# A macaron block on one core: turns through TensorE or through DRAM, and the experts' second product in halves or whole

## The chip, the core and the metric

The kernel runs on one core of a Trainium2 chip. The core has TensorE (matrix products, PE in the profile), VectorE (DVE), ScalarE (ACT), GpSimd (POOL) and SyncE (SP), which issues all DMAs of this kernel. The metric is the device time of one execution in microseconds (us), median of several runs; lower is better.

## The reference

The input `x` has 8 batches of 256 tokens with 128 channels, in float32. Two layers are applied to it, each a half step of a feed-forward, a full step of attention and another half step (all on a normalized x):

```python
x = x + 0.5 * L0_ffn(norm(x))    # soft mixture of 16 experts with 64 slots each
x = x + L0_attn(norm(x))         # linear attention with elu + 1
x = x + 0.5 * L0_ffn(norm(x))    # the same experts again
x = x + 0.5 * L1_ffn(norm(x))    # gated unit with two hidden 512 x 512 products
x = x + L1_attn(norm(x))         # FAVOR+ attention, 16 heads, 32 random features
x = x + 0.5 * L1_ffn(norm(x))

# L0_ffn, with y = norm(x) * g + b and keys se = norm(slot_embeds):
logits = y @ se.T                           # per batch 256 tokens x 1024 slots
slots  = softmax(logits, over tokens).T @ y # 1024 slots x 128
eout   = (gelu(slots @ Wg + bg) * (slots @ Wu + bu)) @ Wd + bd   # per expert
out    = softmax(logits, over slots) @ eout

# FAVOR+: phi = exp(xw - max(xw)) * exp(-|x|^2 / 2) + eps, with xw = heads(x) @ proj
out = (phiQ @ (phiK.T @ V)) / (phiQ @ sum(phiK)), then @ Wo + bo
```

## The kernel before

All of x stays on chip. The batches form two groups of four; a group goes twice through `dispatch`, `experts` and `combine` (after the first time also through `linear`, the linear attention), then through `glu` (two batches at a time), `favor` and `glu` again. `group` (at the end of the kernel's function) writes this down batch by batch.

The order on the engines is not the written one. Each piece of work is a `step` with its engines and their expected costs in ns, the cells that it reads and writes, and a lag until its result can be used. `Plan.place` takes the steps greedily, that which can start first, with ties broken by a key (the TensorE work ahead of the step, plus a shift from the table `SHIFTS`, plus 45 us for the second group), gives out the buffers (`comb`, `slots`, `k1`, `k2`, `k4`, `we`, `sm`, and 8 PSUM banks `ps`) and so fixes each engine's order. SP is one of the engines of the plan: a DMA stands in SP's queue in the planned place and waits there for its data. Where the plan leaves TensorE idle before a step, `Plan.issue` puts in filler matmuls on the identity matrix (L1399 in the profile):

```python
            if s.idle > 700:
                idle(s.bank, int((s.idle - 300) / 224))
```

In `dispatch`, y comes from `norm`; `transposed` turns it (two flips, which are TensorE transposes against the identity, L375) and `affinely` scales it on the way out of PSUM. `replicated` writes y to DRAM in four pieces (L579) and reads it back in four copies of 32 partitions (L586), the layout in which `gathered` (L691) sums tokens into slots on four row tiles of TensorE. The maxima over all slots, which the second softmax needs, are turned (L375), reduced on VectorE (L719) and spread over the partitions by two more flips. GpSimd subtracts them (L737) and ScalarE takes the exponential (L743).

In `experts`, `fetch` brings an expert's matrices (L764) and, for every second expert, the biases of two (L767). `front` makes the gated hidden values (L787 on TensorE, L793, L798). `back` handles two experts at a time: the second product (L818) writes for each batch 64 slots of the first expert to partitions 0 to 63 and 64 slots of the second to 64 to 127, in half-width tiles. One VectorE instruction (L830) adds the bias and writes the result over the slots, where `combine` (L859) reads it.

`squares_turned` is another way to turn a matrix: VectorE transposes within 32 x 32 squares (L446), a DMA writes the result to DRAM (L449), and four DMAs read it back with the squares in turned places (L455). It serves in `linear` and `favor` for the normalized x, in `glu`, and in `favor` for the features of the queries. The attention's outputs in `project` and the FAVOR+ sums in `favor` are turned by flips and copied out of PSUM (L382 on ScalarE, L384 on VectorE).

## Time and profile before

| what | value |
|---|---|
| median of 3 runs | 740.42 us (740.34 to 740.69) |
| the profiled execution's own time | 743.85 us |
| its span, first to last instruction | 742.1 us |
| granted clock of TensorE | 0.998 |
| busy: TensorE, VectorE, ScalarE, GpSimd | 728.8, 517.2, 410.7, 306.1 us |
| DMA: packets, bytes, mean rate | 102105, 62.34 MB, 84 GB/s |
| 32 KB writes of y to DRAM (L579), 64 of them | 1.9 us to landing |
| 128 KB spills of squares (L449), 16 of them | 1.7 us to landing |
| 32 KB moves of squares back (L455), 64 of them | 2.3 us to landing |
| an expert's 384 KB (L764), 64 of them | 3.8 us to landing |

The busy time of an engine is the sum of its instructions' durations; for TensorE their ends are modelled, and the mean duration of a matmul is longer than its distance to the next. The distance between the starts of two groups in the time line is what a group costs.

### The profile page before, as it was taken

The numbers are of one execution on the slowest core, as the hardware profiler recorded it, in microseconds if no ns is written. First come the engines' busy times: TensorE is split into PE (matmuls) and PEld (weight loads), VectorE is DVE, ScalarE is ACT, GpSimd is POOL, SyncE is SP. The second block draws the span as 40 slices with busy tenths as digits, with TensorE's granted clock in tenths as the row PEclk, the third lists the DMA queues.
The fourth block names the chain that finished last, engine by engine and source line by source line (L and its number), as shares of the span: only waits on it lengthen the run. The fifth ranks groups of instructions, "written<-read, shape, count | busy, mean of one in ns | idle before, by whom it ended". The sixth has DMA issues, their size and how long they took to land.

```text
span 742.1 us, 15296 instructions
## 1 busy us (share of the span) xinstructions
PE 728.8 (98%) x5814; PEld 609.5 (82%) x5814; DVE 517.2 (70%) x1103; ACT 410.7 (55%) x774; POOL 306.1 (41%) x419
## 2 busy tenths in 40 slices
PE   8999999998999999999999999999999999999998
PEld 7878888997889988889878879788687677878787
DVE  6999965577868798975564274455998978855442
ACT  4889967257665577884553240433555664363331
POOL 7989446133427752459910022000745545211000
PEclk9999999999999999999999999999999999999999
DMA  5553432333330526333631210200344244120100
GB/s 143 150 140 118 139 93 94 109 81 97 126 114 2 146 83 197 99 94 119 171 99 52 85 29 1 57 0 15 78 114 95 42 118 81 32 60 14 42 1 29
DMA packets 102105, 62.34 MB, mean 84 GB/s; under 512 B 73104, under 2 KB 88848, under 8 KB 102032
## 3 DMA queue, kind: packets, MB, share of 16 engines
q1 hardware_dynamic: 102032, 61.36, 30.6%
q8 instruction: 46, 0.75, 0.4%
q14 instruction: 27, 0.22, 0.1%
HBM read 49.80 MB, written 11.53 MB: 83 GB/s over the span
## 4 chain that ended last, share of the span: by engine, by line
PE 87%; DVE 5%; DMA 3%; SPq 2%; issue 1%; POOL 1%; ACT 1%; POOLq 0%
PE ps L1077 27%; PE ps L787 14%; PE ps L818 8%; PE ps L859 8%; PE ps L691 6%; PE ps L615 4%; PE ps L1177 4%; PE ps L1147 4%; PE ps L1150 4%; PE ps L375 2%; DMA we<-in_We 1%; PE ps L1256 1%; DVE k L632 1%; PE ps L1307 1%; PE ps L1341 1%; PE ps L907 1%
## 5 line engine op out<-in xcount | busy, mean ns | idle before, releaser
L787 PE MATMUL ps<-slots,we 128*128 128x256 f32 x512 | 121.8, 384 | 4.0 <-DMA we<-in_We 2.3
L787 PEld LDWEIGHTS ps<-slots,we 128*128 128x128 f32 x512 | 94.7, 191 | 20.1 <-issue 5.2
L1077 PE MATMUL ps<-comb,slots 128*128 128x256 f32 x448 | 103.1, 381 | 0.0
L1077 PE MATMUL ps<-comb,comb 128*128 128x256 f32 x448 | 102.5, 381 | 0.0
L1077 PEld LDWEIGHTS ps<-comb,slots 128*128 128x128 f32 x448 | 83.6, 190 | 15.4 <-issue 3.9
L1077 PEld LDWEIGHTS ps<-comb,comb 128*128 128x128 f32 x448 | 83.6, 190 | 13.6 <-issue 2.5
L737 POOL TENSOR_TENSOR comb<-comb,k 128x1024 f32<-128x1024 f32 x32 | 75.1, 2369 | 33.5 <-DVE k L384 14.0
L793 ACT ACTIVATE k<-ps,small 128x256 f32<-128x256 f32 x128 | 56.5, 475 | 48.4 <-PE ps L787 46.1
L382 ACT COPY k<-ps 128x512 f32<-128x512 f32 (+2 forms) x55 | 28.5, 519 | 93.8 <-PE ps L1077 83.1
L670 POOL TENSOR_TENSOR comb<-comb,sm 128x1024 f32<-128x1024 f32 x32 | 60.9, 1911 | 41.4 <-DVE sm L665 41.4
L798 DVE SCALAR_TENSOR_TENSOR k<-ps,small,k 128x256 f32<-128x256 f32 x128 | 57.2, 475 | 29.2 <-ACT k L793 28.5
L412 POOL TENSOR_SCALAR sm<-sm 128x2 f32<-128x2 f32 x52 | 10.0, 193 | 153.1 <-DVE sm L406 140.1
L657 ACT ACTIVATE comb<-comb,sm 128x256 f32<-128x256 f32 x128 | 63.3, 497 | 13.7 <-PE ps L691 7.4
L1091 DVE TENSOR_TENSOR comb<-ps,k 128x512 f32<-128x512 f32 x48 | 32.9, 687 | 49.0 <-PE ps L1077 25.5
L818 PEld LDWEIGHTS ps<-we,k 128*64 128x64 f32 x1024 | 55.3, 137 | 9.2 <-issue 4.7
L615 PE MATMUL ps<-k,seT 128*128 128x256 f32 x256 | 61.7, 383 | 0.8 <-DVE k L495 0.5
L818 PE MATMUL ps<-we,k 128*64 128x128 f32 x1024 | 62.2, 275 | 0.0
L691 PE MATMUL ps<-comb,k 32*128 32x256 f32 x1024 | 59.9, 380 | 0.1
L859 PEld LDWEIGHTS ps<-slots,comb 128*128 128x128 f32 x512 | 58.4, 192 | 1.5 <-issue 1.3
L859 PE MATMUL ps<-slots,comb 128*128 128x129 f32 x512 | 59.6, 276 | 0.0
L1099 ACT ACTIVATE comb<-comb 128x512 f32<-128x512 f32 x48 | 30.0, 629 | 51.0 <-DVE comb L1091 50.8
L691 PEld LDWEIGHTS ps<-comb,k 32*128 32x128 f32 x1024 | 51.4, 185 | 5.6 <-issue 1.4
(144 smaller groups left out, 1303.7 us busy)
## 6 DMA issues: line engine op xcount, KB each, us to landing
we<-in_We SPq DMA_DIRECT2D x64, 384.0 KB, 3.8
k<-y SPq DMA_DIRECT2D x64, 128.0 KB, 2.9
t<-comb SPq DMA_DIRECT2D x8, 512.0 KB, 2.8
k<-t SPq DMA_DIRECT2D x32, 128.0 KB, 3.5
y<-k SPq DMA_DIRECT2D x64, 32.0 KB, 1.9
we<-in_bd SPq DMA_DIRECT2D x64, 32.0 KB, 3.6
t<-k SPq DMA_DIRECT2D x16, 128.0 KB, 1.7
k<-t SPq DMA_DIRECT2D x64, 32.0 KB, 2.3
```

The costliest lines, as they stand in the source:

```text
L615: mm(pl.ap[:, j, :], seT[:, 2 * u + j].rearrange("p k s -> p (k s)"), yt.ap, start=True, stop=True,)
L657: nc.scalar.activation(ex.ap[:, 4 * h + j, :], comb.ap[:, 4 * h + j, :], AF.Exp, bias=mx.ap[:, j : j + 1], accum_out=mx.ap[:, 4 + j : 5 + j],)
L670: nc.gpsimd.tensor_tensor(ex.ap[:, part], ex.ap[:, part], mx.ap[:, 8:12].unsqueeze(2).to_broadcast([P, 4, N]), ALU.mult,)
L691: mm(po.ap, yr.ap[rows, c, :], ex.ap[rows, :, 32 * c : 32 * c + 32], start=(c == 0), stop=(c == N // 32 - 1), tile_position=(32 * a, 0),)
L737: nc.gpsimd.tensor_tensor(raw, raw, mb.ap.unsqueeze(1).to_broadcast([P, 4, N]), ALU.subtract)
L787: mm(pe.ap[:, m, :], we.ap[:, ts(2 * m + c, P)], sl.ap[:, j, k, :, 0:S], start=True, stop=True,)
L793: nc.scalar.activation(ga.ap, pe.ap[:, 0, :], AF.Gelu, bias=bg[:, e, c : c + 1])
L798: nc.vector.scalar_tensor_tensor(ht.ap[:, c, :], pe.ap[:, 1, :], bu[:, e, c : c + 1], ga.ap, ALU.add, ALU.mult,)
L818: mm(po.ap[S * k : S * k + S, q, :], hts[k].ap[:, c, ts(q, S)], wes[k].ap[:, ts(4 + c, P)], start=(c == 0), stop=(c == 1), tile_position=( ...
L859: mm(po.ap[:, t, 0 : D + 1], comb.ap[:, j, ts(t, P)], eo()[:, j, q, 0 : D + 1], start=(j == 0), stop=(j == NJ - 1),)
L1077: mm(bank.ap[:, o], w(k)[:, c, ts(o, P)], rhs().rearrange("p (c n) -> p c n", c=2)[:, c, :], start=(start and o + c == 0), stop=(stop and ...
L1091: nc.vector.tensor_tensor(C(i, k)(), bank.ap.rearrange("p o n -> p (o n)"), other(), ALU.add)
```

## The change

- y in one spill: `replicated` writes y by one DMA of 128 partitions and reads it back in four as before, each in pieces of 1 KB instead of 4 KB; `gathered` picks its rows by another index.
- The experts' second product: one expert at a time, with two batches' slots side by side as a full 128-wide stationary side. Each expert's output is added to its bias into a buffer `moved`, and two DMAs place its halves over the slots (64 partitions each). The bias is now part of the matrix `We`, laid out by the host for all 128 partitions, and comes with the same DMA.
- Turns of the outputs in `project` and of the FAVOR+ sums: by `squares_turned`.
- The second layer's y: also by `squares_turned`, into a buffer of its own so that y stays for `replicated`, and scaled afterwards by `affinely`, now from the buffer and not from PSUM.
- The second layer's maxima (`last`): transposed in squares and reduced on VectorE, written to DRAM (4 KB), read back into all partitions (512 KB), and reduced again by two VectorE instructions.
- Costs and lags of SP's steps in the plan have other values, and `SHIFTS` is another table.

The second layer here means the second pass through the experts. The diff, without blank lines and most of `SHIFTS`:

```diff
--- before.py
+++ after.py
@@ -14,19 +14,18 @@
 P = 128
 SHIFTS = (
-    -2751, -1692, -1691, -12195, -784, -1588, -17523, -441, -1660, -895, -929, -659, -543, -591,
...
+    -1808, -823, -822, -570, -566, -619, -564, -372, -388, -402, -161, -439, -208, -237, -230,
...
 )
@@ -437,16 +436,16 @@
         )
         return y
-    def squares_turned(z, n, cells, dst, out):
-        flat = lambda: z()
+    def squares_turned(z, n, cells, dst, out, by=None):
         there = dram.tile([P, n // 32, 32], F32, tag=f"t{len(turns)}", name=f"t{len(turns)}")
         turns.append(there)
-        step({"DVE": 58 + 1.07 * n}, lambda _: nc.vector.transpose(z(), z()), cells, cells)
+        done, at = ([by], lambda: by.ap) if by else (cells, z)
+        step({"DVE": 58 + 1.07 * n}, lambda _: nc.vector.transpose(at(), z()), cells, done)
         def spill(_):
-            nc.sync.dma_start(there.rearrange("p k j -> p (k j)"), z())
+            nc.sync.dma_start(there.rearrange("p k j -> p (k j)"), at())
         def place(_):
@@ -457,8 +456,8 @@
                     squares[f],
                 )
-        step({"SP": 475}, spill, cells, [there.name], lag=1.5 * n)
-        step({"SP": 2000}, place, [there.name], out, lag=2.5 * n)
+        step({"SP": 335}, spill, done, [there.name], lag=1.1 * n - 850)
+        step({"SP": 2400 + 0.7 * n}, place, [there.name], out, lag=1.2 * n - 300)
     turns = []
@@ -469,7 +468,10 @@
             squares_turned(
                 lambda: y.ap[:, 0:n].rearrange("p t d -> p (t d)"), n * P,
                 [(y, t) for t in range(n)], lambda: yt.ap, [yt],
+                Buf("k1", (P, n * P)) if affine else None,
             )
+            if affine:
+                affinely(lambda: yt.ap, lambda: yt.ap, [yt], [yt], n * P, True)
             return yt
         pt = ps_(n, P)
@@ -485,7 +487,7 @@
             evacuated(lambda: yt.ap, flat, [pt], [yt], n * P)
         return yt
-    def affinely(dst, src, r, w, n):
+    def affinely(dst, src, r, w, n, port=False):
         def run(e):
@@ -494,7 +496,7 @@
             else:
                 nc.vector.tensor_scalar(dst(), src(), ng, nb, ALU.mult, ALU.add)
-        step({"ACT": act(n, True) + 87, "DVE": dve(n, 120)}, run, [*r, "ng"], w)
+        step({"ACT": act(n, True) + 87, "DVE": dve(n, 120)}, run, [*r, "ng"], w, port=port)
     def keys():
@@ -568,36 +570,36 @@
     dram = ctx.enter_context(tc.tile_pool(name="dram", bufs=1, space=bass.MemoryType.DRAM))
-    spilled = [dram.tile([32, N // 32, D], F32, tag=f"y{b}", name=f"y{b}") for b in range(B)]
+    spilled = [dram.tile([P, N], F32, tag=f"y{b}", name=f"y{b}") for b in range(B)]
     def replicated(y, b):
         yr = Buf("k4", (P, N // 32, D))
         def spill(_):
-            for k in range(4):
+            nc.sync.dma_start(spilled[b], y.ap.rearrange("p t d -> p (t d)"))
+        def spread(_):
+            blocks = spilled[b].rearrange("(k i) n -> i k n", k=4)
+            for a in range(4):
                 nc.sync.dma_start(
-                    spilled[b].rearrange("i (t k) d -> i k t d", k=4)[:, k],
-                    y.ap[32 * k : 32 * k + 32],
-                )
-        def spread(_):
-            for a in range(4):
-                nc.sync.dma_start(yr.ap[32 * a : 32 * a + 32], spilled[b])
-        step({"SP": 2500}, spill, [(y, t) for t in range(TT)], [("y", b)], lag=-1500)
-        step({"SP": 1765}, spread, [("y", b)], [yr], lag=900)
+                    yr.ap[32 * a : 32 * a + 32].rearrange("i (k t) d -> i k (t d)", t=TT), blocks
+                )
+        step({"SP": 335}, spill, [(y, t) for t in range(TT)], [("y", b)], lag=-500)
+        step({"SP": 1830}, spread, [("y", b)], [yr], lag=900)
         return yr
-    def dispatch(b, sl):
+    def dispatch(b, sl, last):
         plan.part()
         q = b % BG
         y = norm(b, True)
-        yt = transposed(y, TT, True)
+        yt = transposed(y, TT, True, squares=last)
         yr = replicated(y, b)
         if not loaded:
             key, plan.key = plan.key, 60000
@@ -689,7 +691,7 @@
                 for a, po in enumerate(pos):
                     rows = slice(32 * a, 32 * a + 32)
                     mm(
-                        po.ap, yr.ap[rows, c, :], ex.ap[rows, :, 32 * c : 32 * c + 32],
+                        po.ap, yr.ap[rows, TT * (c % 4) + c // 4, :], ex.ap[rows, :, 32 * c : 32 * c + 32],
                         start=(c == 0), stop=(c == N // 32 - 1), tile_position=(32 * a, 0),
                     )
@@ -708,27 +710,64 @@
             nc.vector.tensor_tensor(pm.ap[:, 0], pm.ap[:, 0], pm.ap[:, 1], ALU.max)
         step({"DVE": 330}, fold, [pm], [pm], port=True)
-        pt = ps_(TT, P)
-        mn = Buf("sm", (P, TT))
-        def turn_max(_):
-            for t in range(TT):
-                flip(pt.ap[:, t, :], pm.ap[:, 0, ts(t, P)])
-        def token_max(_):
-            nc.vector.tensor_reduce(mn.ap, pt.ap, AX.X, ALU.max)
-        step({"PE": flips(TT)}, turn_max, [pm], [pt])
-        step({"DVE": dve(N)}, token_max, [pt], [mn])
-        pb = ps_(N)
         mb = Buf("k1", (P, N))
-        def spread(_):
-            for t in range(TT):
-                flip(pb.ap[:, ts(t, P)], mn.ap[:, t : t + 1].to_broadcast([P, P]))
-        step({"PE": flips(TT)}, spread, [mn], [pb], takes=[mb])
-        evacuated(lambda: mb.ap, lambda: pb.ap, [pb], [mb], N)
+        if last:
+            there = dram.tile([P, N // 32], F32, tag=f"m{len(turns)}", name=f"m{len(turns)}")
+            turns.append(there)
+            mn, mr = Buf("sm", (P, N // 32)), Buf("k4", (P, 4, N))
+            def turn_max(_):
+                nc.vector.transpose(pm.ap[:, 0], pm.ap[:, 0])
+            def slot_max(_):
+                nc.vector.tensor_reduce(
+                    mn.ap, pm.ap[:, 0].rearrange("p (c s) -> p c s", s=32), AX.X, ALU.max
+                )
+            def spill(_):
+                nc.sync.dma_start(there, mn.ap)
+            def spread(_):
+                nc.sync.dma_start(
+                    mr.ap.rearrange("p a n -> p (a n)"),
+                    there.rearrange("p c -> (p c)").partition_broadcast(P),
+                )
+            def token_max(_):
+                nc.vector.tensor_tensor(mr.ap[:, 0:2], mr.ap[:, 0:2], mr.ap[:, 2:4], ALU.max)
+                nc.vector.tensor_tensor(
+                    mb.ap.rearrange("p (c i) -> p i c", i=32),
+                    *(mr.ap[:, a].rearrange("p (i c) -> p i c", i=32) for a in range(2)), ALU.max,
+                )
+            step({"DVE": dve(N)}, turn_max, [pm], [pm])
+            step({"DVE": dve(N)}, slot_max, [pm], [mn])
+            step({"SP": 335}, spill, [mn], [there.name], lag=-600)
+            step({"SP": 440}, spread, [there.name], [mr], lag=1300)
+            step({"DVE": 1060}, token_max, [mr], [mb], port=True)
+        else:
...
         for h in range(2):
             half = [(comb, 2 * h), (comb, 2 * h + 1)]
@@ -748,7 +787,7 @@
     def experts(sl):
         def whole(j):
-            return [(sl, j, q) for q in range(BG)]
+            return [(sl, j, k, q) for k in range(2) for q in range(BG)] + [(sl, j, "two")]
         filled = [(sl, "in", q, a) for q in range(BG) for a in range(4)]
@@ -761,18 +800,9 @@
             we = Buf("we", (P, 6 * P + D))
             def run(_):
-                nc.sync.dma_start(we.ap[:, 0 : 6 * P], i["We"][e])
-                if e % 2 == 0:
-                    for k in range(2):
-                        nc.sync.dma_start(
-                            we.ap[S * k : S * k + S, 6 * P :],
-                            i["bd"][e + k].partition_broadcast(S),
-                        )
-            step(
-                {"SP": 475 if e % 2 else 1400}, run, [(sl, "in", BG - 2, 0)], [we],
-                lag=1900 if e % 2 else 1000,
-            )
+                nc.sync.dma_start(we.ap, i["We"][e])
+            step({"SP": 475}, run, [(sl, "in", BG - 2, 0)], [we], lag=1500)
             return we
         def front(e, we):
@@ -807,46 +837,51 @@
                 step({"DVE": dve(256, 59)}, up, [pe, ga], [(ht, c)])
             return ht
-        def back(j, wes, hts):
-            po = ps_(BG, P)
+        def back(e, we, ht):
+            j, k = e // 2, e % 2
+            po = ps_(NB, P)
+            moved = Buf("k1", (P, NB, P))
             def down(_):
-                for q in range(BG):
+                for r in range(NB):
                     for c in range(2):
-                        for k in range(2):
-                            mm(
-                                po.ap[S * k : S * k + S, q, :], hts[k].ap[:, c, ts(q, S)],
-                                wes[k].ap[:, ts(4 + c, P)], start=(c == 0), stop=(c == 1),
-                                tile_position=(0, S * k),
-                            )
-            step(
-                {"PE": 1880}, down,
-                [*wes, *((ht, c) for ht in hts for c in range(2))], [po],
-            )
+                        mm(
+                            po.ap[:, r, :], ht.ap[:, c, ts(r, P)], we.ap[:, ts(4 + c, P)],
+                            start=(c == 0), stop=(c == 1),
+                        )
             def biased(_):
                 nc.vector.tensor_tensor(
-                    eo()[:, j, :, 0:D], po.ap,
-                    wes[0].ap[:, 6 * P :].unsqueeze(1).to_broadcast([P, BG, D]), ALU.add,
-                )
-            step({"DVE": dve(512)}, biased, [wes[0], po], whole(j))
+                    moved.ap, po.ap, we.ap[:, 6 * P :].unsqueeze(1).to_broadcast([P, NB, P]),
+                    ALU.add,
+                )
+            def place(_):
+                for h in range(2):
+                    nc.sync.dma_start(
+                        eo()[S * k : S * k + S, j, h::2, 0:D], moved.ap[S * h : S * h + S]
+                    )
             def twos(_):
                 nc.gpsimd.memset(eo()[:, j, :, D : D + 1], 2.0)
-            step({"POOL": 65}, twos, [], whole(j))
+            cells = [(sl, j, k, q) for q in range(BG)]
+            step({"PE": mms(*[P] * 4)}, down, [we, (ht, 0), (ht, 1)], [po], takes=[moved])
+            step({"DVE": dve(256)}, biased, [we, po], [moved])
+            step({"SP": 1340}, place, [moved], cells, lag=-300)
+            if k:
+                step({"POOL": 65}, twos, [], [(sl, j, "two")])
         got = []
         for e in range(E):
             plan.part()
             we = fetch(e)
             got.append((we, front(e, we)))
-            if e % 2 == 0 and e:
-                back(e // 2 - 1, *zip(*got[e - 2 : e]))
-        back(NJ - 1, *zip(*got[E - 2 :]))
+            if e:
+                back(e - 1, *got[e - 1])
+        back(E - 1, *got[E - 1])
         return eo
     def combine(b, comb, sl, eo):
@@ -863,7 +898,7 @@
             step(
                 {"PE": mms(*[D + 1] * NJ)}, gather,
-                [(comb, u) for u in range(4)] + [(sl, j, q) for j in range(NJ)], [(po, t)],
+                [(comb, u) for u in range(4)] + [c for j in range(NJ) for c in ((sl, j, 0, q), (sl, j, 1, q), (sl, j, "two"))], [(po, t)],
             )
         rc = Buf("sm", (P, TT))
@@ -887,15 +922,10 @@
     def project(b, oh, w):
-        pt = ps_(TT, P)
         ot = Buf("k1", (P, N))
-        def turn(_):
-            for t in range(TT):
-                flip(pt.ap[:, t, :], oh.ap[:, t, :])
-        step({"PE": flips(TT)}, turn, [oh], [pt], takes=[ot])
-        evacuated(lambda: ot.ap, lambda: pt.ap.rearrange("p t c -> p (t c)"), [pt], [ot], N)
+        squares_turned(
+            lambda: oh.ap.rearrange("p t d -> p (t d)"), N, [oh], lambda: ot.ap, [ot]
+        )
         projected_onto(b, ot, w)
     def projected_onto(b, ot, w):
@@ -1297,7 +1327,7 @@
             [(phi, 0, c) for c in range(4)],
             lambda: qk.ap.rearrange("p a b n -> p (a b n)"), [(qk, t) for t in range(TT)],
         )
-        pk, pkt = ps_(2, P), ps_(2, P)
+        pk = ps_(2, P)
         kvm = Buf("k1", (P, 2, P))
         def sums(_):
@@ -1317,17 +1347,13 @@
                 m4of.unsqueeze(1).unsqueeze(3).to_broadcast([P, 2, 4, M]), ALU.mult,
             )
-        def turn_sums(_):
-            for m in range(2):
-                flip(pkt.ap[:, m, :], kvm.ap[:, m, :])
         step(
             {"PE": 1020}, sums, [*((phi, 1, c) for c in range(4)), v1], [pk], takes=[kv, kvm]
         )
         step({"DVE": 340}, blocks, [pk], [kvm])
-        step({"PE": flips(2)}, turn_sums, [kvm], [pkt])
-        evacuated(
-            lambda: kv.ap, lambda: pkt.ap.rearrange("p a (c n) -> p a c n", c=4), [pkt], [kv], N
+        squares_turned(
+            lambda: kvm.ap.rearrange("p a n -> p (a n)"), N, [kvm],
+            lambda: kv.ap.rearrange("p a c n -> p (a c n)"), [kv],
         )
@@ -1367,7 +1393,7 @@
         bs_ = range(g * BG, (g + 1) * BG)
         for layer in range(2):
             sl = Buf("slots", (P, NJ, 2, BG, S1))
-            combs = {b: dispatch(b, sl) for b in bs_}
+            combs = {b: dispatch(b, sl, layer > 0) for b in bs_}
             eo = experts(sl)
             for b in bs_:
                 combine(b, combs[b], sl, eo)
@@ -1452,10 +1478,10 @@
                 get(f0 + "Wg"),
                 get(f0 + "Wu"),
                 wd.reshape(wd.shape[0], 2, P, P).transpose(0, 2, 1, 3).reshape(-1, P, 2 * P),
+                np.broadcast_to(get(f0 + "bd")[:, None, :], (wd.shape[0], P, P)),
             ],
             axis=2,
         ),
-        "bd": get(f0 + "bd"),
         "WqkvT": get("L0_attn_Wqkv").T,
         "WprojT": get("L0_attn_Wproj").T,
         "bproj": get("L0_attn_bproj"),
```

## The prediction

> **What bounds the kernel now.** I read the page's busy shares, then the chain that ended last, then the time line of TensorE group by group, then SyncE's queue, then the busy time by stage.
>
> The page and its chain of waits:
>
> ```profile
> PE 728.8 (98%) x5814; PEld 609.5 (82%) x5814; DVE 517.2 (70%) x1103; ACT 410.7 (55%) x774; POOL 306.1 (41%) x419
> ...
> PEclk9999999999999999999999999999999999999999
> ...
> PE 87%; DVE 5%; DMA 3%; SPq 2%; issue 1%; POOL 1%; ACT 1%; POOLq 0%
> ...
> L787 PE MATMUL ps<-slots,we 128*128 128x256 f32 x512 | 121.8, 384 | 4.0 <-DMA we<-in_We 2.3
> ```
>
> TensorE carries 87% of the chain at full clock. "98% busy" alone would not prove it, since ends of pipelined matmuls are modelled; the distance between starts does. From the time line of TensorE (start, us, engine, line, operation, count):
>
> ```profile
> 317.41 1.89 PE L787 MATMUL ps<-slots,we 128*128 128x256 f32 x8
> 319.14 0.38 PE L375 MATMUL ps<-ident,k 128*128 128x128 f32 x2
> 319.36 1.89 PE L787 MATMUL ps<-slots,we 128*128 128x256 f32 x8
> ...
> 354.93 5.34 PE L787 MATMUL ps<-slots,we 128*128 128x256 f32 x24
> 360.21 1.97 PE L818 MATMUL ps<-we,k 128*64 128x128 f32 x32
> 362.10 1.99 PE L787 MATMUL ps<-slots,we 128*128 128x256 f32 x8
> 363.94 1.03 PE L1147 MATMUL ps<-k,w1T 128*128 128x512 f32 x2
> ...
> 691.89 3.73 PE L1177 MATMUL ps<-w3T,comb 128*128 128x128 f32 x32
> 695.46 1.02 PE L1147 MATMUL ps<-k,w1T 128*128 128x512 f32 x2
> ```
>
> Prices, start to start: a 128x256 instruction is 1.73/8 = 0.216 us, a flip (transpose by matmul) 0.22/2 = 0.11, a full-array 128x128 instruction 3.57/32 = 0.112. (A full-array float32 matmul of the program is two instructions in the trace, a flip one.) The 32 instructions of the experts' second product (L818) take 1.89. The neighbours pay as well: the 24 before it take 5.28 instead of 24 x 0.216 = 5.18, the 8 after it 1.84 instead of 1.73, about 0.10 us on each side of a change of tile shape.
>
> With these prices and the program's order I add up TensorE. The full-array and narrow work without changes of shape is 701 us, of which 43 filler matmuls (L1399) are 9.6; 130 changes of shape at 0.10 are 13.0; another 0.08 for each of 28 visits to L818 (1.89 against 2 x 1.785 = 3.57 for two in a row, which the time line gives as 3.65) is 2.2. Total 716 of the span of 742.1. The other 26 us are 7 in the start-up before 61.6 us (9.6 of fillers stand there too), 1.6 before the first matmul, 3.3 after the last, and about 14 of small waits. The largest wait, again in the time line:
>
> ```profile
> 179.13 1.03 PE L787 MATMUL ps<-slots,we 128*128 128x256 f32 x4
> 182.32 1.46 PE L787 MATMUL ps<-slots,we 128*128 128x256 f32 x4 [2.17 <-DMA we<-in_We]
> 183.57 0.64 PE L375 MATMUL ps<-ident,k 128*128 128x128 f32 x2
> 184.00 1.92 PE L787 MATMUL ps<-slots,we 128*128 128x256 f32 x4
> 185.71 0.95 PE L972 MATMUL ps<-kv,k 128*128 128x129 f32 x4
> ```
>
> and SyncE's queue before it:
>
> ```profile
> 168.02 3.04 SPq L579 DMA_DIRECT2D y<-k  x4
> 171.56 2.58 SPq L455 DMA_DIRECT2D k<-t  x4
> 174.24 0.55 SPq L764 DMA_DIRECT2D we<-in_We  x1
> 174.83 1.16 SPq L767 DMA_DIRECT2D we<-in_bd  x2
> 176.03 0.58 SPq L764 DMA_DIRECT2D we<-in_We  x1
> ```
>
> An expert's weights were issued behind spills and square moves and came late. The wait is 2.2 us, but the eight 128x256 instructions and two flips around it then ran at up to twice their price (184.00 to 185.71 for four of them, 1.71 instead of 0.86): about 4 us in all. So an idle of 2 us costs two of slow matmuls on top.
>
> **The change, part by part.** TensorE first.
>
> Flips. Three turns go to squares through DRAM: the second layer's y (8 x 2 flips), the outputs in `project` (8 x 2), the FAVOR+ sums (8 x 2); and the second layer's maxima lose two flips to turn and two to spread (8 x 4). 80 flips x 0.109 = 8.7 us less.
>
> Second product. Before: 32 calls, each 32 half-width instructions, 1.785 us without the borders. After: 64 calls of 4 full-array matmuls, 8 instructions x 0.1117 = 0.893. That is 57.1 against 57.2: nothing by itself. The gain is the borders: in the order of the changed program the changes of shape fall from 130 to 89, 41 x 0.10 = 4.1, and the 28 x 0.08 = 2.2 go. 6.3 us less. The row first: 0.0558 us per half-width instruction, 0.1117 per full one, with equal work. The Trainium skill speaks against this edit: TensorEngine Tiling (Array Packing), Overview, "Theoretical Speedup", promises up to 2x from tiles where a dimension is at most 64, and the old form has 64 stationary columns. If that were a gain that is given up, the new form would cost twice, 57 us more. But the two batches' slots are now joined into one stationary side of 128 columns, so the array is as full as before; the sum by the rule's own premise is 0, and I take the row.
>
> Fillers. The plan puts 48 instead of 43, +5 x 0.223 = +1.1 us: 38 instead of 43 in the start-up, and three new places later (2, 5 and 3): before the first combine, between the first layer's linear attention and the experts, and before an expert's second product in the middle. Line 211 sets a filler count only where the plan idles over 0.7 us, and leaves 0.3 us each: +0.9.
>
> TensorE's sum: -8.7 - 6.3 + 1.1 + 0.9 = -13.0 us.
>
> SyncE's queue, in issue times. New: 128 placements of expert outputs, 64 rows each. No row has that shape; the nearest two are a 32 KB spill of 64 rows (0.593) and a square move (0.612), so between 0.33 (a 128-row spill) and 0.7, taken 0.67 for its 128 pieces: +86. 24 more spills at 0.33 and 96 more square moves at 0.62: +67. The maxima, 8 x (0.33 + 0.44): +6. y's spread in 1 KB pieces instead of 4 KB: 64 x 0.04 = +2. Gone: 64 bias loads at 0.58, -37 (the bias rides in `We`, 448 KB each instead of 384), and y's four spills become one, 16 x (2.4 - 0.33) = -33. In sum 238 us to 330. Between the first combine and the second layer's last one about 152 us of issuing fall into some 200 us, three quarters of the queue.
>
> Here the skill has a rule against the change: DMA: Bandwidth & Descriptors, "Rules for kernel authors": many small transfers should be joined, since under 64 KB one pays mostly overhead. The row agrees on the price (a 32 KB square move is 0.61 to issue and 2.3 to land, a 128 KB spill 0.33 and 1.7). Charged as elapsed time by the page's fixed cost of about 2 us, the net 152 added DMAs would be +304 us, an estimate. By the trace they overlap each other and TensorE, so only what arrives late counts; before, with 238 us of issuing, late `we` cost about 5 us (182 and 216 us).
>
> What is queued behind a placement: it waits for `biased` on VectorE, which waits for the second product, and the next experts' `we`, other batches' squares and y's spreads wait behind it on SP. Its reader is `gather` (L859 before), which needs all 16 experts. After the last second product of a stage, `biased` 0.42, two issues 1.3 and a landing of about 2 make 4 us where it was 0.7. The changed order puts L693 (3.67), other batches' glu or logits between, and the 2 fillers at the first combine: covered. If the cover is gone: four combines x 3.3 = 13 us.
>
> Latency of the squares: transpose 0.43, spill 0.33 + 1.7, four moves 2.5, landing 2.3 and, for y, the affine 0.55, some 8 us against 0.8 through PSUM, in 24 places. Covered by the other group's experts and by the glu (TensorE has no wait over 1 us from 300 on). The maxima take some 7 us longer and are due only at the combine.
>
> VectorE: the second product's add becomes 64 x 0.42 for 32 x 0.69, +5; transposes 24 x 0.43, +10; the maxima 8 x (0.43 + 0.41 + 1.3 - 0.41), the last pair bounded by 0.69 and by 0.61 each, +14; about half the copies out of PSUM go, -7. +22, to 539, 74%. The stage that matters:
>
> ```profile
> 0.00:61.60 61.60, 56.46 (x477) 47.29 (x478) 55.00 (x123) 44.33 (x123) 54.70 (x90) 1.00 0.59 158
> ...
> 190.00:300.00 110.00, 108.63 (x1008) 95.27 (x1008) 90.50 (x208) 76.17 (x160) 54.71 (x78) 1.00 0.38 109
> ```
>
> From 190 to 300 us VectorE (fifth number) works 90.5 of 110; about 9 to 10 of the 22 fall here, so 100 of the 106 that are left. Close, not over.
>
> In the start-up VectorE has 55 of 61.6 us, and the change takes nothing off it; y's single spill lands 2 us earlier. Gain 0 to 2, taken 0.5.
>
> New waits from a fuller SP queue and a tighter VectorE: at least -3 (the delay at 182 us stood behind four y spills, which shrink by 2.7 us), at most +16 (four like that at 182); taken +3, rather more than half of what `we` cost before.
>
> Sum: 742.1 - 13.0 - 0.5 + 3 = 731.6. The profiled execution took 743.85 with a span of 742.1; the median of the runs is 740.42, 1.7 below the span. So 730 us.
>
> **The rivals.**
> (a) VectorE is the bound from 190 to 300 us. It keeps that stage at 110 and passes some waits on, so the 4 us of TensorE saved there are lost and 2 to 3 more: 736. For it: 82% busy before. Against: 100 < 106, and the fillers planned there are only 8.
> (b) The gain is only exchanged for waits, 740: flips were cheap fill while TensorE waited. For it: fillers in three new places. Against: flips stand between matmuls without idle.
> (c) Slower: SP is the bound between the first combine and the second layer's last. Each in-order placement holds back `we`; when a `we` comes 2 us late, 4 us are lost, as at 182 us. It decides from four such events (16 us) on; five give 740.4 - 16 + 20 = 744. For it: three quarters full, placements that wait for VectorE in the same queue. Against: y's spills and the bias loads are out of that queue, and each weight has four buffers.
> (d) It doesn't do what it says: if the full-array product still drained at each border, the 6.3 would stay: 736.
>
> **How the numbers follow.** My forecast (725 to 734) 0.52, (a) or (d) 0.25, (b) 0.09, (c) 0.12, better than 725 0.02. 0.2% is 1.5 us, about what a measurement can tell from no change. Faster: 0.79; same: 0.09; slower: 0.12. The range reaches from 724 (fewer waits than before) to 741 (end of (b)) and leaves out (c) and a little below.
>
> **What would show it.** Right: 48 flips on k and 16 on sm; L850 with 8 instructions from start to start in 0.89 and the next 128x256 group at 0.216; TensorE's share of the chain near 87%; no idle over 1.5 us after the start-up but the planned three. Wrong: rows "PE <- DMA we" or "PE <- DMA slots" of over 5 us together, matmuls at twice their price after them, VectorE on the chain between 190 and 300 us with over 10%.

## The result, and the profile after

| | before | after |
|---|---|---|
| median | 740.51 us (740.34 to 740.69, 4 runs) | 769.31 us (767.71 to 770.90, 4 runs) |
| ratio | | 1.0389, 95% interval 1.0364 to 1.0413 |
| span of the profiled execution | 742.1 us | 765.5 us |
| TensorE not busy in the span | 13.3 us | 41.2 us |
| TensorE instructions | 5814 | 5232 |

The change made the kernel 3.9% slower; 730 us was predicted. From the page of after, in its order: busy times, the clock by slices, the shares of the chain that ended last, and the group of the experts' first product:

```profile
PE 724.3 (95%) x5232; PEld 608.2 (79%) x5232; DVE 533.8 (70%) x1161; ACT 429.3 (56%) x788; POOL 309.7 (40%) x417
...
PEclk9999999999999999999999999999999999999999
...
DMA packets 150615, 83.29 MB, mean 109 GB/s; under 512 B 101136, under 2 KB 138384, under 8 KB 150544
...
PE 66%; DMA 14%; DVE 9%; SPq 4%; POOL 2%; ACT 2%; issue 2%; DVEq 0%; ACTq 0%; POOLq 0%
...
L817 PE MATMUL ps<-slots,we 128*128 128x256 f32 x512 | 122.5, 384 | 18.2 <-DMA we<-in_We 14.1
```

TensorE's share of the chain fell from 87% to 66%, and the DMAs' rose from 3% to 14%. The granted clock stayed full in the mean (0.996, before 0.998), so the time did not go into a slower TensorE as a whole. The first product (L817, L787 before) now stands idle 18.2 us instead of 4.0, mostly until an expert's weights have landed.

The work itself fell nearly as predicted. In the time line of TensorE (start, us, engine, line, operation, count), the whole-array second product is L850:

```profile
419.79 0.59 PE L817 MATMUL ps<-slots,we 128*128 128x256 f32 x2
420.22 1.05 PE L850 MATMUL ps<-we,k 128*128 128x128 f32 x8
421.11 1.89 PE L1107 MATMUL ps<-comb,comb 128*128 128x256 f32 x8
422.84 1.05 PE L850 MATMUL ps<-we,k 128*128 128x128 f32 x8
```

Eight instructions take 421.11 - 420.22 = 0.89 us from start to start, and the eight 128x256 ones after them 1.73, their full price: no border is left. I added up the distances between TensorE's starts in both traces, without the waits and the stretches at half clock: the work fell by some 11.0 of the predicted 13.0 us (an estimate). Still the span grew by 23.4, so 34.4 us came on top. Three parts make them up:

- 41.2 - 13.3 = 27.9 us are more idle time.
- 4.6 us belong to the same waits. There are 51 of them instead of 24, and the matmul before each counts as busy up to its modelled end, some 0.17 us beyond its price (0.384 against 0.216).
- 1.9 us are matmuls at half clock. The trace has two stretches of 3.4 us at a granted clock of 0.50 (49.8 and 206.8 us) where before had one (183.0).

TensorE's waits by their releaser (waiting line, releaser: us in total, times, longest):

```profile
PE ps L817 <- DMA we<-in_We: 14.1, 13, 3.7
PE ps L937 <- DMA k<-t: 4.4, 4, 2.0
PE ps L817 <- DVE k L828: 2.7, 1, 2.7
PE ps L617 <- ACT k L495: 2.4, 2, 2.2
PE ps L1367 <- DMA kv<-t: 2.2, 1, 2.2
```

By releaser, and against before, the idle grew by 11.8 us for weights (`we`), 7.9 for turned tiles, 5.3 for VectorE and 2.4 for ScalarE. The weights are the largest, but three of the other rows are turns through DRAM: `project` waits for turned outputs (L937), FAVOR+ for turned sums (L1367), and the logits (L617) for L495, which scales the turned y of the second layer. Before, the first row was 2.3 us, and no wait for a turned tile was over 0.3.

SyncE's queue at one place of after, with the weights that TensorE waits for:

```profile
174.31 6.32 SPq L454 DMA_DIRECT2D k<-t  x8
180.74 0.55 SPq L803 DMA_DIRECT2D we<-in_We  x1
181.39 1.30 SPq L863 DMA_DIRECT2D slots<-k  x2
182.79 0.54 SPq L803 DMA_DIRECT2D we<-in_We  x1
...
197.68 0.54 SPq L732 DMA_DIRECT2D k<-m  x1
198.32 0.40 SPq L803 DMA_DIRECT2D we<-in_We  x1
198.81 1.60 SPq L863 DMA_DIRECT2D slots<-k  x2
200.46 0.61 SPq L803 DMA_DIRECT2D we<-in_We  x1
201.12 0.57 SPq L448 DMA_DIRECT2D t<-k  x1
201.79 0.38 SPq L581 DMA_DIRECT2D y<-k  x1
202.27 0.49 SPq L803 DMA_DIRECT2D we<-in_We  x1
```

TensorE there, and then two steps of the chain that ended last (start, us, what):

```profile
201.27 1.03 PE L817 MATMUL ps<-slots,we 128*128 128x256 f32 x4
206.00 1.31 PE L817 MATMUL ps<-slots,we 128*128 128x256 f32 x4 [3.70 <-DMA we<-in_We]
```

```profile
198.32 7.64 DMA we<-in_We
206.00 1.31 PE ps L817 x4
```

Eight moves of turned squares hold the queue for 6.3 us, and weights, placements (L863) and other moves follow closely. But the weights that end the wait of 3.70 us were issued at 198.32, before TensorE ran dry, and took 7.64 us to land. Just before them stood the 512 KB of a batch's maxima (L732). From 202 to 206 us the 16 DMA engines are full (busy shares of 0.98 and 1.02 in two windows of 2 us, up to 359 GB/s). So at the largest wait the queue's order is not all: the transfer itself was slow. The same is true of the wait of 2.17 us before, which the prediction put down to a late issue: its weights left at 176.03 and took 6.25 us.

How long weights take to land, from the issue to the arrival of the data (L764 before, L803 after; minimum, median and maximum in us), before and after:

```profile
DMA to landing us min/median/max: 2.9/3.8/6.6
```

```profile
DMA to landing us min/median/max: 3.2/4.6/7.6
```

The plan counted the other way. A fetch was counted until its lag's end as 475 + 2000 + 1900 = 4375 ns (with the two biases 1400 + 2000 + 1000 = 4400), and is now 475 + 2000 + 1500 = 3975 ns (2000 ns is the plan's general lag of a SyncE step). The old value stood above the median landing; the new one stands 0.6 us below it.

The spill of the turns (L449 before, L448 after) has the same pattern:

```profile
DMA to landing us min/median/max: 1.7/2.0/3.4
```

```profile
DMA to landing us min/median/max: 1.7/2.5/6.5
```

The change has 56 of these spills for 32, and it also tells the plan that each is quicker. Up to its lag's end a spill of 256 columns counted 475 + 2000 + 1.5 x 256 = 2859 ns before and 335 + 2000 + 1.1 x 256 - 850 = 1767 ns now. The old value stood above the median landing, the new one stands near the minimum. The four moves stand right behind the spill in a queue that keeps its order, so where the spill is late SyncE itself waits. These are the rows of SyncE's waits for it, before and after:

```profile
SPq L455 <- DMA t<-k: 16.1, 11, 2.5
```

```profile
SPq L454 <- DMA t<-k: 40.8, 26, 3.9
```

So three suspects stand: the placements in SyncE's queue, the load that the turns and the maxima put on the queue and on the DMA engines, and the shorter lags.

### The profile page after: what moved, and what is told of

Same layout as the page of the kernel before. It is cut to its first block, busy times and chain, and to the rows that moved or that the text cites. A ratio compares the mean times of both kernels' runs of the same rounds, so it can differ in the third digit from the quotient of the medians.

```text
span 765.5 us, 14599 instructions
## 1 busy us (share of the span) xinstructions
PE 724.3 (95%) x5232; PEld 608.2 (79%) x5232; DVE 533.8 (70%) x1161; ACT 429.3 (56%) x788; POOL 309.7 (40%) x417
## 4 chain that ended last, share of the span: by engine, by line
PE 66%; DMA 14%; DVE 9%; SPq 4%; POOL 2%; ACT 2%; issue 2%; DVEq 0%; ACTq 0%; POOLq 0%
PE ps L1107 25%; PE ps L817 8%; DMA we<-in_We 5%; PE ps L850 4%; PE ps L1207 4%; PE ps L1177 4%; PE ps L1180 4%; PE ps L693 3%; PE ps L894 3%; PE ps L617 3%; DMA k<-m 2%; DMA k<-t 2%; DMA t<-k 2%; SPq L454 2%; DVE comb L680 1%
## 5 line engine op out<-in xcount | busy, mean ns | idle before, releaser
L817 PE MATMUL ps<-slots,we 128*128 128x256 f32 x512 | 122.5, 384 | 18.2 <-DMA we<-in_We 14.1
L817 PEld LDWEIGHTS ps<-slots,we 128*128 128x128 f32 x512 | 93.6, 190 | 36.6 <-DMA we<-in_We 12.2
L828 DVE SCALAR_TENSOR_TENSOR k<-ps,small,k 128x256 f32<-128x256 f32 x128 | 57.0, 477 | 24.9 <-ACT k L823 24.5
L850 PEld LDWEIGHTS ps<-we,k 128*128 128x128 f32 x512 | 63.4, 192 | 6.1 <-issue 2.2
L617 PE MATMUL ps<-k,seT 128*128 128x256 f32 x256 | 62.6, 390 | 4.5 <-ACT k L495 2.4
L850 PE MATMUL ps<-we,k 128*128 128x128 f32 x512 | 65.1, 276 | 0.9 <-DVE k L828 0.8
L617 PEld LDWEIGHTS ps<-k,seT 128*128 128x128 f32 x256 | 48.0, 194 | 12.7 <-ACT k L495 3.4
```

The lines of the kernel that those rows point to most:

```text
L617: mm(pl.ap[:, j, :], seT[:, 2 * u + j].rearrange("p k s -> p (k s)"), yt.ap, start=True, stop=True,)
L817: mm(pe.ap[:, m, :], we.ap[:, ts(2 * m + c, P)], sl.ap[:, j, k, :, 0:S], start=True, stop=True,)
L828: nc.vector.scalar_tensor_tensor(ht.ap[:, c, :], pe.ap[:, 1, :], bu[:, e, c : c + 1], ga.ap, ALU.add, ALU.mult,)
L850: mm(po.ap[:, r, :], ht.ap[:, c, ts(r, P)], we.ap[:, ts(4 + c, P)], start=(c == 0), stop=(c == 1),)
```

## The experiments

The first theory, rival (c) of the prediction, was that the placements in SyncE's queue hold back the weights. Its rivals: the load of the turns and maxima, and the order written with too short lags. Where a kernel changes the plan, it has a table `SHIFTS` of its own, searched with one method and like effort; how much such a table decides by luck is measured at the end. All ratios are against before on the same chip, with the 95% interval; "idle" is the span less TensorE's busy time in the profiled execution.

| run | median, us | ratio | idle, us |
|---|---|---|---|
| e1_place_act | 772.96 | 1.0435 (1.0388 to 1.0482) | 43.3 |
| e2_place_pool | 768.81 | 1.0361 (1.0301 to 1.0421) | 40.0 |
| e3_direct | 761.10 | 1.0265 (1.0237 to 1.0293) | 35.9 |
| e4_product_alone | 741.85 | 1.0010 (0.9989 to 1.0031) | 16.1 |
| e5_old_product | 770.46 | 1.0394 (1.0335 to 1.0453) | 39.5 |
| e6_true_lags | 756.34 | 1.0220 (1.0188 to 1.0252) | 25.5 |
| e7_relieved | 738.13 | 0.9959 (0.9944 to 0.9974) | 10.9 |
| e8_outputs | 760.52 | 1.0278 (1.0253 to 1.0302) | 30.4 |
| e9_y2 | 748.60 | 1.0116 (1.0091 to 1.0142) | 16.7 |
| e10_maxima | 746.08 | 1.0073 (1.0042 to 1.0105) | 18.4 |
| e11_sums | 755.67 | 1.0204 (1.0162 to 1.0247) | 22.3 |
| e12_only_lags | 748.06 | 1.0099 (1.0083 to 1.0115) | 18.0 |
| e13_old_lags | 760.81 | 1.0273 (1.0258 to 1.0289) | 32.2 |
| e14_two_turns | 743.58 | 1.0042 (1.0028 to 1.0057) | 16.1 |
| e15_direct | 743.86 | 1.0053 (1.0038 to 1.0068) | 18.4 |
| e16_doubled | 768.73 | 1.0377 (1.0362 to 1.0393) | 34.8 |
| e17_relieved_again | 744.02 | 1.0053 (1.0034 to 1.0071) | 12.7 |
| e18_only_lags_again | 756.86 | 1.0198 (1.0153 to 1.0243) | 22.2 |

### The placements

The changed kernel in its own order, with the placements issued by ScalarE, and by GpSimd:

```diff
-                    nc.sync.dma_start(
+                    nc.scalar.dma_start(      # e1_place_act
+                    nc.gpsimd.dma_start(      # e2_place_pool
```

> The changed kernel with one edit: the 128 DMAs that place the experts' outputs are issued from ScalarE's queue instead of SyncE's, at the same places of the same plan; the order on TensorE, VectorE and GpSimd stays. Theory 1 (SP's in-order queue is full, about 330 us of issuing with most of it between 110 and 380 us, and the experts' weights are issued late behind placements and squares): SP loses 77 us of issuing and its waits for placements; most of the 26 us that TensorE waits for the weights go, ScalarE gains 77 us of issuing (429 to about 506 of 745), and the time falls to 742 to 752. Theory 2 (the DMA engines are the limit: more bytes and more small packets, landings of 2.4 instead of 1.7 us for a spill, 4.6 instead of 3.8 for weights): the traffic is the same, so landings stay at 2.4 and 4.6 us and the time stays at 765 to 771. Theory 3 (the plan's order is worse whatever the queues do): 765 to 771 as well, with TensorE waiting for other things than the weights.

> The changed kernel with the 128 placements issued from GpSimd's queue instead of SyncE's, in the same plan. Theory 1: the weights come on time as in the run with ScalarE's queue, but GpSimd's own work (310 us) gets 128 issues and stands behind VectorE's results[...]; 745 to 765. Theory 2 and 3: 765 to 775. A time over 770 would say that GpSimd's queue has become the bound instead.

Neither came near before's time. On ScalarE the 128 issues stand among its activations. TensorE's waits of e1_place_act:

```profile
PE ps L850 <- DVE k L828: 7.2, 6, 3.8
PE ps L817 <- DMA we<-in_We: 6.4, 11, 1.8
PE ps L937 <- DMA k<-t: 4.7, 4, 1.6
PE ps L894 <- DMA slots<-k: 3.0, 1, 3.0
```

The waits for weights halve (14.1 to 6.4 us; the 26 us of the expectation counts the same waits twice, for matmuls and for weight loads), and a wait for VectorE takes their place: L828 needs the gelu from ScalarE, which now stands behind placements that wait for their data. On GpSimd the waits for weights fall to 4.0 us without a matching gain. The placements land later than from SyncE: 3.6 us from ScalarE and 2.9 from GpSimd against 2.4. The Trainium skill says (DMA: Bandwidth & Descriptors, "Issuing engines are not separate DMA queues") that all issuers run on the same 16 DMA engines, so another issuer saves only the sequencer's time. Here even that saving did not show in the time (772.96 and 768.81 us against 769.31), so SyncE's time for issuing placements is not the bound. Both runs fit full DMA engines as well as an unfit order.

Next the placements were taken away, the order kept: VectorE writes the two halves over the slots itself. In this kernel the first half's write comes before the next expert has read its slots, so the second expert of each pair works on overwritten slots: its values differ from the reference, the amount of work does not.

```diff
-                nc.vector.tensor_tensor(
-                    moved.ap, po.ap, we.ap[:, 6 * P :].unsqueeze(1).to_broadcast([P, NB, P]),
-                    ALU.add,
-                )
+                    nc.vector.tensor_tensor(
+                        eo()[S * k : S * k + S, j, h::2, 0:D], po.ap[S * h : S * h + S],
+                        we.ap[S * h : S * h + S, 6 * P :].unsqueeze(1).to_broadcast([S, NB, P]),
+                        ALU.add,
```

> The changed kernel without the 128 placement DMAs, in the same plan: two VectorE instructions of 64 partitions (instead of one of 128) add the bias and write each expert's output straight from PSUM over the slots, from partitions 0 to 63 to 64 to 127 where needed; SyncE's queue keeps everything else in its order. It takes away both the issue time (86 us of SP) and the traffic (8.4 MB) of the placements, and puts 64 more instructions (27 us) on VectorE. If the placements are the cause, by their queue or by their traffic, the time falls to 738 to 752. If the squares of y, of the outputs and of the sums, and the maxima are the cause (their longer way to data that TensorE needs), the time stays at 758 to 770, with TensorE waiting for DMA k<-t and for the weights as before. If VectorE is the bound in the middle, it gets slower than 769.

Without the 128 DMAs there is 8 us to gain from 769.3, and 35.9 us of idle stay. The largest wait in this kernel is its own, TensorE 5.7 us for those writes, so the placements took some 8 to 14 us of the 28.8 in this order (an estimate, the upper end without these new waits). They are not the bulk.

The two halves of the change, the product on before alone (with the bias in `We`), and the changed kernel with the old product, each with its own table (the cut shows only the head of the changed function):

```diff
-        def back(j, wes, hts):
+        def back(e, we, ht):      # e4_product_alone, on before
-        def back(e, we, ht):
+        def back(j, wes, hts):    # e5_old_product, on the changed kernel
```

> The kernel before with one part of the change: the whole-array second product with its 128 placement DMAs, and the bias in We. Turns, y in four spills and the maxima stay as before. The plan is made anew with a table of shifts searched for this kernel. TensorE loses about 6 us of borders; SP has 238 + 86 - 37 = 287 us of issuing. If the placements are what fills the queue: 748 to 762, with TensorE waiting over 10 us for the weights. If the turns through DRAM are: 734 to 742.

> The changed kernel with the second product of before (half-width tiles, two experts at a time, the add straight over the slots, no placements), the biases of two experts packed into We; y in one spill, all turns through DRAM and the maxima through DRAM stay. Its own plan, searched in the same way. SP has about 244 us of issuing, as much as before, TensorE 8.7 us less than before. If the placements are the cause: 733 to 743. If the turns and the maxima are: 752 to 766, with TensorE waiting for DMA k<-t and for VectorE behind DMA k<-m.

The first theory does not hold. The product with all its placements leaves the time at before's (with y's spills still in four pieces), and taking it out of the changed kernel moves nothing that the intervals would show. With the weights' short lag of 1500 in place, e4_product_alone gets them almost in time:

```profile
PE ps L779 <- DMA we<-in_We: 2.9, 6, 0.8
```

### The lags

The changed kernel, planned with the landings that its trace shows (the lags of y's spill, the placements and the maxima grow as well, and are cut here):

```diff
-        step({"SP": 335}, spill, done, [there.name], lag=1.1 * n - 850)
-        step({"SP": 2400 + 0.7 * n}, place, [there.name], out, lag=1.2 * n - 300)
+        step({"SP": 335}, spill, done, [there.name], lag=1.1 * n + 150)
+        step({"SP": 2400 + 0.7 * n}, place, [there.name], out, lag=1.2 * n + 100)
...
-            step({"SP": 475}, run, [(sl, "in", BG - 2, 0)], [we], lag=1500)
+            step({"SP": 475}, run, [(sl, "in", BG - 2, 0)], [we], lag=2800)
```

> The changed kernel, all parts, but the plan is told the landings that the changed kernel's trace shows (weights 4.8 us instead of 3.5, spills 2.4 instead of 1.4, y's spill 3.2 instead of 1.5, placements 2.5 instead of 1.7, the maxima's two transfers 2.5 and 4.3 instead of 1.4 and 3.3), with a table of shifts searched for it. If the order was the fault, made for landings that the loaded queue does not keep: 740 to 752. If the load itself is (the queue full between 150 and 380 us, whatever the order): 757 to 770.

13 us are back, but not all. The waits for weights fall from 14.1 to 3.8 us. The next kernel, called the relieved one, is before with only what takes load off SyncE: y in one spill, and the bias in `We`.

```diff
-            for k in range(4):
-                nc.sync.dma_start(
-                    spilled[b].rearrange("i (t k) d -> i k t d", k=4)[:, k],
-                    y.ap[32 * k : 32 * k + 32],
-                )
+            nc.sync.dma_start(spilled[b], y.ap.rearrange("p t d -> p (t d)"))
...
-                nc.sync.dma_start(we.ap[:, 0 : 6 * P], i["We"][e])
+                nc.sync.dma_start(we.ap, i["We"][e])
```

> The kernel before with only what takes work off SyncE's queue: y in one spill and the bias in We (packed by pairs, 64 fewer DMAs); 238 - 33 - 37 = 168 us of issuing. Its own searched plan. If the queue costs time in the kernel before as well (5 us of late weights): 733 to 738. If not: 738 to 742. Over 742 would say that the searched table is a worse one than the kernel's own.

With this table it is the fastest kernel of this study. On it the parts were put one at a time, those of squares with the changed lags:

```diff
+        squares_turned(               # e8_outputs
+            lambda: oh.ap.rearrange("p t d -> p (t d)"), N, [oh], lambda: ot.ap, [ot]
+        )
+        yt = transposed(y, TT, True, squares=last)      # e9_y2
+        if last:                      # e10_maxima: spilled and spread, lags of turns as before
+        squares_turned(               # e11_sums
+            lambda: kvm.ap.rearrange("p a n -> p (a n)"), N, [kvm],
```

> The relieved kernel (738.1: the kernel before with y in one spill and the bias in We) plus one part: the outputs in project turn by squares through DRAM, with the changed kernel's costs and lags for squares. Own searched plan. TensorE saves 1.75 us; SP gets 8 x 2.8 = 22 us more. If the turns that lie on the way from the first to the second pass through the experts are the cause: 744 to 756, with TensorE waiting for DMA k<-t. If the maxima are the cause: 735 to 740. If it takes all of them together to fill the queue: 736 to 741.

> The relieved kernel plus one part: the second layer's y turns by squares, into its own buffer, and is scaled afterwards. TensorE saves 1.75 us. If the way from the first to the second pass is the cause: 744 to 756, with TensorE waiting for the scaling behind DMA k<-t. If the maxima are: 735 to 741. If only all together: 736 to 741.

> The relieved kernel plus one part: the second layer's maxima through DRAM (two VectorE steps, 4 KB out, 512 KB back, two more VectorE instructions). TensorE saves 3.5 us, VectorE gets about 14 us. If the maxima are the cause (the 512 KB land in 4.2 us instead of the plan's 3.3, and GpSimd's subtraction and the softmax wait): 746 to 760. If the turns of outputs and y are: 733 to 740.

> The relieved kernel plus one part: the FAVOR+ sums turn by squares. TensorE saves 1.75 us. They lie after 460 us, where the changed kernel's TensorE waits little: 735 to 740 by every theory but one, that the changed costs and lags of all squares (a spill planned to land after 1.4 us instead of 2.4) are themselves the fault: then 742 to 752, since this kernel too plans the 32 squares of before with them.

All four are slower than the relieved kernel, by 22.4, 10.5, 7.9 and 17.5 us. These can't be added up, since three of them carry the lags too. The control has the lags of the turns alone: no operation is changed, only two lines of the plan and with them the table.

```diff
-        step({"SP": 475}, spill, cells, [there.name], lag=1.5 * n)
-        step({"SP": 2000}, place, [there.name], out, lag=2.5 * n)
+        step({"SP": 335}, spill, cells, [there.name], lag=1.1 * n - 850)
+        step({"SP": 2400 + 0.7 * n}, place, [there.name], out, lag=1.2 * n - 300)
```

> The relieved kernel (738.1) with no work changed: only the two lines of costs and lags of squares_turned are those of the changed kernel (a spill of 256 columns is planned to land 1.77 us after its issue begins instead of 2.86), and the table is searched anew. If these numbers are the fault, because the moves back then stand at the head of SyncE's queue and wait for a spill that lands late: 748 to 758, with SyncE waiting over 35 us in L455's place for DMA t<-k. If the added turns are: 736 to 741.

9.9 us more, with the same work. SyncE's waits for the spills reach the changed kernel's 40.8 us although there are 32 turns and not 56:

```profile
SPq L457 <- DMA t<-k: 40.0, 22, 5.7
```

The reverse is the changed kernel with the old lags of the squares, and then two of the turns on the relieved kernel, with the old lags:

```diff
-        step({"SP": 335}, spill, done, [there.name], lag=1.1 * n - 850)
-        step({"SP": 2400 + 0.7 * n}, place, [there.name], out, lag=1.2 * n - 300)
+        step({"SP": 475}, spill, done, [there.name], lag=1.5 * n)
+        step({"SP": 2000}, place, [there.name], out, lag=2.5 * n)
...
+        squares_turned(               # e14_two_turns: these two, on the relieved kernel
+            lambda: oh.ap.rearrange("p t d -> p (t d)"), N, [oh], lambda: ot.ap, [ot]
+        )
...
+        squares_turned(
+            lambda: kvm.ap.rearrange("p a n -> p (a n)"), N, [kvm],
```

> The changed kernel with all its parts, but the two lines of costs and lags of squares_turned as before; searched table. If these numbers are the fault: 738 to 750 (its other lags, for the placements, y's spill and the maxima, stay tight). If the load on the DMA path is: 757 to 770.

> The relieved kernel with the turns of the outputs and of the FAVOR+ sums through DRAM, planned with the costs and lags of before; searched table. TensorE saves 3.5 us. If the numbers in the plan are the fault of the slow runs with one turn each (760.5 and 755.7): 733 to 741. If the turns themselves are: 752 to 765.

With old lags the changed kernel gains 8.5 us (769.3 to 760.8). Outputs and sums together, 16 turns more, run in 743.6 us, where each alone with the short lags took 760.5 and 755.7. One row speaks against the wait of SyncE as the whole mechanism: e14_two_turns has `SPq L457 <- DMA t<-k` at 39.2 us, as high as the slow kernels, and only 16.1 us of idle on TensorE. What seems to count is whether anything that TensorE needs soon stands behind; no run tests that by itself.

### The load, and the luck of a table

A whole-array product written directly by VectorE, now ordered after all readers, on the relieved kernel:

```diff
+                for h in range(2):
+                    nc.vector.tensor_tensor(
+                        eo()[S * k : S * k + S, j, h::2, 0:D], po.ap[S * h : S * h + S],
+                        we.ap[S * h : S * h + S, 6 * P :].unsqueeze(1).to_broadcast([S, NB, P]),
+                        ALU.add,
+                    )
```

> The relieved kernel with the whole-array second product, whose results two VectorE instructions of 64 partitions write straight over the slots (after the next expert has read its own), so without placements; squares as before; searched table. TensorE loses about 6 us of borders, VectorE gains 64 x 0.84 - 32 x 0.69 = 32 us (516 to 548). If the borders are worth what I took them for: 730 to 736. If VectorE's 32 us cost as much: 736 to 742.

No gain: VectorE is busy 546.3 us and has 15% of the chain, and 4.3 us of waits for weights remain.

The load alone, with plan, table and work of the other engines kept: after each turn's moves four more of the same shape, into memory that nothing reads. And two kernels with a second, independent table.

```diff
+        again = dram.tile([P, n], F32, tag=f"u{len(turns)}", name=f"u{len(turns)}")
...
+            for f in range(4):
+                nc.sync.dma_start(
+                    again[32 * f : 32 * f + 32].rearrange("p (t a j) -> p t a j", a=4, j=32),
+                    squares[f],
+                )
```

> The relieved kernel (738.13 us), same plan and table of shifts, but each turn by squares through DRAM (32 of them) is followed by four more moves of the same shape from DRAM to DRAM, into memory that nothing reads: 128 more DMAs on SyncE's queue, at about 0.61 us of issue each 79 us more of SyncE, and 4 MB more traffic. TensorE's, VectorE's and ScalarE's work and their order are unchanged. Theory 'load': what the turns cost is SyncE's time and the traffic themselves, so the time rises by 8 to 18 us, to 746 to 756 us, with new TensorE waits for weights or turned tiles. Theory 'plan alone': the work was covered and only the order written for too short lags costs; the time stays under 741 us.

> The relieved kernel again, with a second table of shifts, searched independently with the same effort. It tells how much of a difference between two planned kernels is the luck of their tables. Theory 'luck is small': 735 to 742 us against 738.13 us of the first table. Theory 'luck is large': 745 us or more, so that differences of 8 to 10 us between planned kernels prove nothing.

> The relieved kernel with only the two lines of cost and lag of the turns by squares changed to the new values (no work is changed), with a second table of shifts, searched independently. The first table gave 748.06 us, 9.9 us above the relieved kernel. Theory 'the short lag costs': 744 to 753 us again. Theory 'the first table was unlucky': 736 to 741 us.

The 128 added DMAs cost 30.6 us (768.73 against the relieved kernel's 738.13, with the same table), though none of their data is used. SyncE's queue and TensorE's time line in e16_doubled (L464 are the added moves, L459 the true ones):

```profile
254.69 1.27 SPq L459 DMA_DIRECT2D k<-t  x2
256.00 2.57 SPq L464 DMA_DIRECT2D u<-t  x4
258.68 0.55 SPq L453 DMA_DIRECT2D t<-k  x1
260.63 2.54 SPq L459 DMA_DIRECT2D k<-t  x4
263.21 2.57 SPq L464 DMA_DIRECT2D u<-t  x4
```

```profile
256.35 0.61 PE L907 MATMUL ps<-WprojT,k 128*128 128x128 f32 x4
265.12 1.20 PE L928 MATMUL ps<-WqkvT,k 128*128 128x128 f32 x4 [8.16 <-DMA k<-t]
266.10 1.06 PE L932 MATMUL ps<-k,WqkvT 128*128 128x256 f32 x2
266.96 1.06 PE L936 MATMUL ps<-WqkvT,k 128*128 128x128 f32 x4
267.95 2.75 PE L818 MATMUL ps<-we,k 128*64 128x128 f32 x32
270.63 0.71 PE L928 MATMUL ps<-WqkvT,k 128*128 128x128 f32 x4
```

The next turn's spill (L453) is issued only after the added moves, at 258.68; its moves end at 263.17, and TensorE starts at 265.12 after 8.16 us of idle. In the relieved kernel the wait at this place is 1.71 us. Then the matmuls cost up to twice their price: four 128x128 ones 0.98 us instead of 0.44, the second product 2.68 instead of 1.89. From 265.12 to 270.63 us that makes 5.5 us for work of 3.2 (0.44 + 0.43 + 0.44 + 1.89).

Against the relieved kernel, TensorE's idle grew by 34.8 - 10.9 = 23.9 us and the span by 30.8. Slow matmuls explain most of the rest: the granted clock is 0.50 here for 10.2 us, idle time included, and for 3.4 us at two later places (593.9 and 655.3 us); by the distances between starts the three cost 5.9 us.

The Trainium skill has this as a rule (TensorE: Matmul & The Clock Gate, Part 1): the clock is halved after about 3.4 us of idle, until as long a busy time has passed. The factor agrees, and the slow matmuls here last about 4.4 us (2.83, and twice the 0.79 that the second product lost). The length of the idle does not decide as simply: before had the half clock after 2.17 us, while a wait of 3.50 us in e16_doubled (172.46 us) left the clock at 1.00. Of the six waits of 2 us or more in after, two were followed by it (48.6 and 206.0 us).

The controls put the sizes in order. A second table moves the relieved kernel by 5.9 us (738.1, 744.0) and the one with short lags by 8.8 (748.1, 756.9). So between two planned kernels a difference below some 9 us proves nothing: neither that the relieved kernel beats before, nor the costs found for the maxima or the direct write, nor that the placements of e4_product_alone are free; y's 10.5 us lie on the border.

What of the short lags? Both tables with them are above both with the old (means 752.5 and 741.1, 11.4 us apart). Two tables each are few: the smallest difference between the pairs is 4.0 us, and if tables were luck alone, this order would still come up one time in six. Other comparisons point the same way: longer lags gave the changed kernel 8.5 us (turns alone) and 13.0 (all lags), and two turns with old lags took 12 to 17 us less than one of them with short ones. So a cost of the short lags is likely, and its size is not known better than 4 to 19 us. Outputs and sums with short lags are beyond the luck of a table (12 to 22 us above the two relieved tables), but against the lags alone they are between 12 us more and 1 us less, so how much the turns add is not told.

## Why the prediction was wrong

- Right in the main: the work that leaves TensorE. No border is left at L850, eight instructions of it take 0.89 us, and TensorE has 5814 - 5232 = 582 instructions less: 512 of the second product and 80 flips less, and 10 for five fillers more. Some 11 of the 13.0 us went.
- Right: the mean clock stays full, and VectorE (rival (a)) does not decide, although TensorE's waits for it grew by 5.3 us. In windows of after (us; PE, PEld, DVE, ACT and POOL busy; clock, DMA share, GB/s) VectorE works 10 to 14 of 20 us where TensorE waits most, and is nearly full only where TensorE is too:

```profile
180.00:200.00 20.00, 15.35 (x89) 13.09 (x90) 13.53 (x29) 13.77 (x31) 5.78 (x10) 1.00 0.77 170
200.00:220.00 20.00, 16.30 (x125) 13.85 (x126) 10.41 (x23) 10.16 (x14) 5.00 (x4) 0.91 0.64 179
220.00:240.00 20.00, 19.33 (x169) 17.47 (x168) 19.44 (x39) 16.68 (x43) 10.62 (x12) 1.00 0.59 156
```

- Wrong, by 1 us: the start-up. The first expert's product was to start half a us earlier; it starts at 62.04 us, before at 61.57.
- Wrong, and the step that failed: the term "New waits from a fuller SP queue and a tighter VectorE", taken at +3 us with an upper end of +16. The runs show some 34 us in its place, 32.5 of waits and 1.9 of slow matmuls. It was sized by one sort of wait, late weights, and scaled from the 5 us before. That sort alone grew by 11.8 us: the prediction named the 448 KB, but neither that they would land later (4.6 us for 3.8) nor that the plan now counted on 3.98 us instead of 4.4. The other sort, "Latency of the squares", was put at nothing, since TensorE had no wait over 1 us there before; waits for turned tiles grew by 7.9 us. Their cover had been made by an order that counted 2.86 us for each spill. The change to 1.77 us stands in the diff, and the prediction gave it no price.
- How far the short lags are the cause is not shown. The turns' lags are likely to cost, somewhere between 4 and 19 us; the weights' lag was put back only together with all others (e6). By itself it does not do it: the relieved kernel and e4_product_alone have the same short lag, with no row and with 2.9 us of waits for weights.
- Too general: "an idle of 2 us costs two of slow matmuls on top", read from one place. In after no slow matmuls followed four of the six waits of 2 us or more.
- Rival (c) had the right side and the right rows (`PE <- DMA we` of over 5 us together, matmuls at twice the price), at a chance of 0.12 and with 744 us. Its mechanism, placements that hold back the weights, was too narrow: placements on another queue or product taken out (e1, e2, e5) leave 769 to 773 us, taking out the DMAs alone (e3) gains 8, and the placements alone, with an order planned for them (e4), cost nothing beyond the luck of a table.
- The rule that the prediction weighed, that many small transfers pay mostly overhead (DMA: Bandwidth & Descriptors, "Rules for kernel authors"), pointed the right way. With the same page's fixed 2 us for a DMA, which it gives for those issued from GpSimd, the estimate for 152 added DMAs was 304 us; the trace shows some 34 us on top, so most of the DMAs stay covered. The prediction took the row's issue price and left the row's lateness out; the truth lay between, nearer to the row.

Not settled: with the old lags of the turns or with measured lags the changed kernel still takes 756 to 761 us, 12 to 23 above the two tables of the relieved kernel, which do neither the added turns nor the maxima nor the placements. e16_doubled shows that load of this kind can cost that much, but in an order that didn't know of it, and it loads SyncE's queue and the DMA engines at once. How the rest divides among turns, maxima and placements, and between the queue and the DMA engines, these runs don't tell. The changed kernel as it stands has one table only, so up to some 9 of its 28.8 us may be that table's luck.
